# Router logits from the turned tokens and eight more columns of the second feed forward matrix, instead of turns of the normalised rows

## The chip, the cores and the metric

The kernel runs on one core of one Trainium2 chip. The core has a matrix engine (TensorE, PE in the profile; its weight loads are listed apart as PEld), a vector engine (VectorE, DVE), a scalar engine (ScalarE, ACT), GpSimd (POOL), and SyncE (SP), which here mostly issues transfers. On-chip data lies in SBUF, 128 partitions wide. Matmuls write to PSUM, which has eight banks of 512 float32 values for each partition. The metric is device time in microseconds, the median of several runs.

## The reference, cut to what matters

Two images of 256 channels and 56 by 56 pixels go through a convolutional neighbourhood attention (layer 0) and then, as 6272 tokens of 256 channels, through a linear attention with a feed forward part and through a mixture of eight experts (layer 1). The change lies in layer 1, between the feed forward part and the router:

```
# t: 6272 tokens of 256 channels; ln = (x - mean) / sqrt(var + 1e-5)
xn  = ln(t)                                     # input of the linear attention
msg = ln(attention(xn) @ Wm) * g1 + b1
h   = relu(concat([xn, msg]) @ W1)
t   = t + xn + ln(h @ W2) * g2 + b2             # token after the attention layer
x2  = ln(t)                                     # input of the experts
probs   = softmax(x2 @ Wr + br)                 # 8 experts
top_p, top_idx = top_k(probs, 2)
weights = top_p / sum(top_p)
xe  = ln(x2) * ln_g[e] + ln_b[e]
y   = gelu(xe @ W1[e] + b1[e]) @ W2[e] + b2[e]
out = t + sum of the two chosen y, weighted
```

The router needs `x2 @ Wr`. Since `x2` is `(t - mean) * r`, and a token `t` is the old token plus `xn` plus the feed forward result, the logits can also be summed from `xn @ Wr` and `h @ (W2 * g2) @ Wr`, if the columns of `Wr` are centred first.

## The kernel before, in words

**Stages.** The profile's span has three parts. Up to about 780 us the function `front` does the convolutions and the neighbourhood attention, and at its end `first_keys` starts the linear attention's keys for the first image. From about 780 to 1340 us `layer1` runs the linear attention, the feed forward part and the router over groups of tokens, and in its last quarter already the first expert tiles. From 1340 us on the remaining expert tiles run (`Experts.run`, lines 1388 to 1433).

**Tiles.** Tokens come in blocks of 128 rows. `order` (line 1452) has 14 groups: eleven of four blocks, two of two blocks, and one of a single block.

**The pipeline.** The loop at line 1830 takes steps s = 0 to 17. In step s, `queries` handles group s, `message` group s-1, `feed_forward` group s-2, `route` group s-3, and in steps 0 to 5 two `keys` generators handle blocks of the second image. Each of them is a generator that yields between parts. The strings `turns` and `last` (lines 1818 to 1823) are the order written out by hand in which the parts are taken: q, m, f, r, u and v (keys), p (what is left of the previous step's `route`), c (shared set-up of the experts) and e (a part of an expert tile). `manual_schedule` holds TensorE to this order. The orders of the other engines are set beforehand by a planner, which works with its own costs and takes first what is marked `high_priority`; every engine works its queue in order.

**What a group does.** `keys` (line 266) normalises two blocks (`stats`, `rstd`, `norm`), turns them (TensorE transposes into `pts`, copied by `evac` into `xT`) and forms the keys; on GpSimd it also replaces the stored token by token + normalised token + b2 (lines 286 to 289). `queries` multiplies `xT` by `w_q` and divides by a denominator. `message` forms `pm`, normalises it (`rms`, `rstd`, a ScalarE multiply) and turns it. `feed_forward` (line 1658) makes four tiles `p1` (16 matmuls of up to 512 columns, ScalarE Relu into `hT`), and then per two blocks eight matmuls into one bank `py` of 2 times 256 columns (line 1678), the sums of squares (`rms`, ScalarE), `rstd` (VectorE scale, then a power on GpSimd), `u` = py times its scale and g2 (VectorE, line 1687), the addition to the token (GpSimd, line 1691) and a write of the token to `y2` by SyncE. `route` (line 1732) takes statistics of the new token, normalises it twice in one go into `row`, turns `row` with eight transposes and two copies (lines 1755 to 1761), and in its second part multiplies the turned rows by `wr`, eight columns wide (line 1766); `top_two` picks the experts in some twenty small VectorE operations, the third part counts slots with two matmuls into `pp`, and the rest scatters the rows to their slots in device memory (`xs`) by GpSimd's indirect transfers.

**PSUM in this part.** `ps_h` has three banks for `pm`, `p1`, `py` and one of the expert accumulators (`py2`); `ps_q` two (queries, turned messages, expert `ph`); `ps_a` two (keys, `pts`, `pl`, `pp`); `ps_k` one. A tile waits until all readers of the bank's previous tile are done.

**Weights.** `layer1` loads its constants with GpSimd-issued transfers (`load`, line 1464). `prepare_feed_forward` centres the columns of W2 (`fw2`) after step 0. A matmul of float32 appears in the profile as two records, a transpose as one.

## Time and profile before

| what | value |
|---|---|
| median of 3 runs | 2046.03 us (2042.52 to 2046.82) |
| the profiled execution: its own time, its span | 2042.29 us, 2040.5 us |
| mean granted TensorE clock | 0.975 |
| busy in the span: PE, PEld, DVE, ACT, POOL | 92%, 66%, 50%, 31%, 33% |
| chain that ended last: PE, DVE, DMA, POOL | 66%, 14%, 6%, 5% |
| TensorE busy, 780 to 840 us | 54.82 of 60 us |
| TensorE busy, 1340 to 2040 us | 675.86 of 700 us |
| first and last `py` of the feed forward (L1678) | 845.3 and 1305.5 us |

A line of the timeline reads: start in us, duration in us, engine, line of the kernel, operation, output <- inputs with shapes, how many instructions were merged, and in brackets how long the engine had been idle before and what ended that. A line of the windows reads: stretch, its length, then busy time and number of instructions of each engine, the granted clock, the transfers' share and their rate. The durations of merged TensorE lines include the pipeline's depth; the time that a run of matmuls takes from the queue is the distance to the next line's start.

### The profile page before, as it was taken

What the parts mean: (1) busy time and instruction counts of PE and PEld (TensorE: products, weight loads), DVE (VectorE), ACT (ScalarE), POOL (GpSimd) and SP (SyncE); (2) the same over time, 40 slices, a digit from 0 to 9 for tenths busy, and PEclk for the clock granted to TensorE, in tenths of its full rate; (3) what the DMA queues carried; (4) which work ended last, traced back from release to release, by engine and by line L of the source; (5) the groups of instructions that cost most, each with busy time, mean ns of one, the idle gap of its engine ahead of it and who ended that gap; (6) DMA issues with size and microseconds to landing.
All of it is one profiled execution on the core that took longest, in us unless ns stands there. A gap on an engine that the chain in (4) does not pass through costs nothing.

```text
span 2040.5 us, 27636 instructions
## 1 busy us (share of the span) xinstructions
PE 1882.0 (92%) x10102; PEld 1342.9 (66%) x10102; DVE 1020.2 (50%) x2483; ACT 623.8 (31%) x1228; POOL 680.4 (33%) x772
## 2 busy tenths in 40 slices
PE   4999898999777888999999999999999999999995
PEld 2545454554445555666656667888888888888885
DVE  4987988877875566355555554342212221221121
ACT  1333334323232222333332323322222222222332
POOL 4532110121033235346344445533233332333221
PEclk9999899999889899999999999999999999999998
DMA  5542432344412224001011143577666767666995
GB/s 117 151 109 74 144 111 71 101 137 112 149 44 65 51 52 155 11 11 50 35 43 54 42 140 104 165 202 211 201 193 188 196 189 205 189 196 194 294 274 158
DMA packets 189911, 264.65 MB, mean 130 GB/s; under 512 B 26424, under 2 KB 149638, under 8 KB 189520
## 3 DMA queue, kind: packets, MB, share of 16 engines
q1 hardware_dynamic: 160912, 220.82, 35.5%
q0 software_dynamic: 20576, 29.75, 7.6%
q10 hardware_dynamic: 8272, 12.15, 1.7%
q8 instruction: 84, 1.38, 0.3%
q14 instruction: 67, 0.55, 0.1%
HBM read 196.38 MB, written 70.55 MB: 131 GB/s over the span
## 4 chain that ended last, share of the span: by engine, by line
PE 66%; DVE 14%; DMA 6%; POOL 5%; issue 3%; ACT 3%; SPq 1%; DVEq 0%; POOLq 0%; ACTq 0%
PE ph L1404 15%; PE py L1422 15%; PE pc L549 6%; PE py L528 5%; PE p L1666 5%; PE po L609 4%; PE s_ps L364 2%; DVE yc L567 2%; POOL rs L263 2%; PE s_ps L599 2%; DMA y<-yt,idi 2%; DVE p L604 2%; DMA xr<-xs 2%; PE kx L307 2%; PE kp L294 2%
## 5 line engine op out<-in xcount | busy, mean ns | idle before, releaser
L1404 PE MATMUL ph<-xe,w1e 128*128 128x256 f32 (+1 forms) x1696 | 362.6, 371 | 3.7 <-DVE xe L1380 2.5
L1422 PE MATMUL py<-w2e,hT 128*128 128x256 f32 x1616 | 359.0, 379 | 0.0
L1408 ACT ACTIVATE hT<-ph,sv 128x256 f32<-128x256 f32 (+1 forms) x424 | 196.5, 464 | 499.1 <-PE ph L1404 496.3
L1404 PEld LDWEIGHTS ph<-xe,w1e 128*128 128x128 f32 x1696 | 310.3, 191 | 46.1 <-DVE xe L1380 3.8
L1422 PEld LDWEIGHTS py<-w2e,hT 128*128 128x128 f32 x1616 | 302.5, 190 | 38.7
L567 DVE SCALAR_TENSOR_TENSOR yc<-ypad,w,yc 128x1120 f32<-128x1120 f32 x192 | 266.5, 1389 | 32.3 <-ACT yc L562 28.9
L161 POOL DMA_INDIRECT y<-yt,idi x101 | 160.8, 1592 | 230.2 <-DVE yt L1428 135.8
L549 PE MATMUL pc<-ypad,diag 128*128 128x448 f32 x432 | 176.8, 548 | 1.0 <-ACT ypad L534 1.0
L1360 DVE CAST idi<-xr 128x2 int32<-128x2 f32 (+1 forms) x53 | 10.5, 199 | 300.3 <-DMA xr<-xs 295.8
L528 PE MATMUL py<-t_a,wq 128*128 128x448 f32 (+1 forms) x384 | 150.1, 527 | 10.6 <-DVE t_a L503 10.3
L1428 DVE SCALAR_TENSOR_TENSOR yt<-py,eq,yt 128x256 f32<-128x256 f32 x101 | 48.6, 483 | 217.6 <-PE py L1422 217.4
L603 ACT ACTIVATE p<-s_ps 112x952 f32<-112x952 f32 (+5 forms) x88 | 102.1, 1160 | 148.2 <-PE po L609 81.2
L604 DVE TENSOR_TENSOR p<-p,tab 112x952 f32<-112x952 f32 (+5 forms) x88 | 125.1, 1425 | 30.6 <-ACT p L603 30.6
L263 POOL TENSOR_TENSOR rs<-rs,mhalf 128x2 f32<-128x2 f32 (+2 forms) x89 | 66.5, 753 | 217.5 <-DVE rs L262 155.2
L517 POOL TENSOR_SCALAR diag<-ident,w 128x128 f32<-128x128 f32 x108 | 89.1, 845 | 142.2 <-PE pc L549 125.4
L549 PEld LDWEIGHTS pc<-ypad,diag 128*128 128x128 f32 x432 | 79.8, 191 | 69.6 <-issue 64.4
L1386 POOL TENSOR_SCALAR yt<-b2e,eq 128x256 f32<-128x256 f32 x101 | 47.4, 478 | 218.8 <-DMA b2e<-in_L_ffn_b 212.6
L528 PEld LDWEIGHTS py<-t_a,wq 128*128 128x128 f32 x384 | 70.6, 194 | 75.0 <-issue 58.8
L161 POOL DMA_INDIRECT xs<-row,si x98 | 96.5, 985 | 58.3 <-DVE si L1790 26.4
L609 PE MATMUL po<-p,v 98*32 98x170 f32 (+5 forms) x960 | 77.0, 376 | 38.8 <-DVE p L604 17.1
L1666 PE MATMUL p<-m2T,fw 128*128 128x512 f32 (+2 forms) x224 | 93.9, 542 | 0.0
L1678 PE MATMUL py<-fw,hTl 128*128 128x256 f32 x392 | 88.5, 381 | 0.0
(364 smaller groups left out, 2550.0 us busy)
## 6 DMA issues: line engine op xcount, KB each, us to landing
w1e<-in_L_ffn_W SPq DMA_DIRECT2D x53, 1024.0 KB
w2e<-in_L_ffn_W SPq DMA_DIRECT2D x53, 1024.0 KB
yd<-yc SPq DMA_DIRECT2D x24, 784.0 KB
ld<-yd SPq DMA_DIRECT2D x28, 448.0 KB
xr<-xs SPq DMA_DIRECT2D x48, 260.0 KB
b2e<-in_L_ffn_b SPq DMA_DIRECT2D x53, 128.0 KB
yr<-y SPq DMA_DIRECT2D x11, 512.0 KB
td<-t_i SPq DMA_DIRECT2D x24, 224.0 KB
```

Source lines behind the costliest of these rows:

```text
L161: ins = nc.gpsimd.indirect_dma_start(out=dst[:, :], out_offset=bass.IndirectOffsetOnAxis(ap=index, axis=0), in_=src, in_offset=None, **kw,)
L263: newest[1] = nc.gpsimd.tensor_tensor(r[:, :n], r[:, :n], mhalf[:, :n], ALU.pow).ins
L528: nc.tensor.matmul(py[:, :n, :], wq1[:, ct, oc * P : (oc + 1) * P], x_sb[:, ct, (q0 + g0) * WW : (q0 + g0 + n) * WW], start=(ct == 0), sto ...
L549: nc.tensor.matmul(pc, diag[:, tap, :], ypad[:, dy : dy + 8, dx : dx + WW], start=(tap == 0), stop=(tap == 8),)
L567: nc.vector.scalar_tensor_tensor(yc[:, 8:, :], src, w, yc[:, 8:, :], ALU.mult, ALU.add)
L603: nc.scalar.activation(p[:nk, :, :n], s_ps[:nk, :, :n], AF.Exp)
L604: nc.vector.tensor_tensor(grid(p), grid(p), table[:nk], ALU.mult)
L609: nc.tensor.matmul(dst[hs] if w is None else den[hs], v[:nk, hs] if w is None else w[:nk, :], grid(p)[:, h, :, o : o + q.shape[2]], start= ...
L1404: nc.tensor.matmul(p1, x.w1[:, ct, j * P : (j + 1) * P], x.xe[:, ct, :], start=(ct == 0), stop=(ct == 1),)
L1408: nc.scalar.activation(hT[:, j, :], p1, AF.Gelu, bias=x.sv[:, 4 + j : 5 + j])
L1422: nc.tensor.matmul(py, hT[:, j, h * P : (h + 1) * P], x.w2[:, j, :], start=(j == 0), stop=(j == NJ - 1),)
L1666: nc.tensor.matmul(p1[:, :w], fw1[:, k, oc * P : (oc + 1) * P], rhs, start=(k == 0), stop=(k == 3))
```

## The change

The rows are no longer turned for the router. Part by part:

- `rstd` keeps variance + eps beside its result, and `keys` passes a place in a new tile `tk.up` (one value per token) into which GpSimd multiplies the two: the old token's standard deviation.
- W2 and g2 get eight more columns: `fw2` is 4 x 264, `g2` 264 wide with ones at its end. A new generator `prepare_router` runs in three parts (x) in step 1: it centres `wr`, scales it by g2 and by b2 (new tile `g2b2`, two small transfers), turns `fw2` with eight transposes and two copies, multiplies the turned matrix by the scaled `wr`, and copies the result into the eight columns.
- In `feed_forward` a block's `py` is 264 wide and has a bank of its own, so that two blocks take two banks; `u` carries the eight columns along, and a small addition makes `lb`.
- `wr` is padded to 32 columns. `route` multiplies it, as the stationary side, with the turned tokens `xT` that the keys made: block k writes partitions 32k to 32k+31 of one bank `pa`; one copy `la` and one transpose give the logits in `pl`.
- `top_two` has two more operations (times 1 + deviation, plus `lb`).
- Smaller: `xt` and `st` are smaller, `mn` has two buffers instead of three, and the order string of step 1 has three x.

```diff
-    def rstd(sm, var, scale):
+    def rstd(sm, var, scale, deviation=None):
         n = var.shape[1]
-        r = sm.tile([P, 4], F32, name="rs")
+        r = sm.tile([P, 2, 4], F32, name="rs")
...
+        if deviation is not None:
+            nc.gpsimd.tensor_tensor(deviation, r[:, 0, :n], r[:, 1, :n], ALU.mult)
+        return r[:, 0, :]
...
+            fw2 = wp.tile([P, 4, C + E], F32, name="fw2")
...
+            wr = wp.tile([P, 2, 32], F32, name="wr")
+            nc.gpsimd.memset(wr, 0.0)
...
+            def prepare_router():
+                ps = ps_a.tile([P, 512], F32, name="wrm", tag="a")
+                for ct in range(2):
+                    nc.tensor.matmul(ps[:, :E], ones, wr[:, ct, :E], start=(ct == 0), stop=(ct == 1))
...
+                yield
+                pt = [ps_a.tile([P, 512], F32, name="fwt", tag="a") for _ in range(2)]
+                f2T = wk.tile([P, 2, 512], F32, name="f2T", tag="qz")
+                for ct in range(2):
+                    for kk in range(4):
+                        nc.tensor.transpose(
+                            pt[ct][:, kk * P : (kk + 1) * P], fw2[:, kk, ct * P : (ct + 1) * P], ident
+                        )
+                    evac(f2T[:, ct, :], pt[ct])
+                yield
+                ps = ps_a.tile([P, 512], F32, name="fwr", tag="a")
+                for kk in range(4):
+                    for ct in range(2):
+                        nc.tensor.matmul(
+                            ps[:, kk * E : (kk + 1) * E], f2T[:, ct, kk * P : (kk + 1) * P], wg[:, ct, 0, :],
+                            start=(ct == 0), stop=(ct == 1),
+                        )
...
                 for k0 in range(0, n, 2):
                     kn = min(2, n - k0)
-                    py = ps_h.tile([P, 2, C], F32, name="py", tag="h")
+                    pys = []
                     for k in range(kn):
+                        py = ps_h.tile([P, 512], F32, name="py", tag="h")
+                        pys.append(py)
                         c0 = (k0 + k) * P
                         for kk in range(4):
                             nc.tensor.matmul(
-                                py[:, k, :], hT[:, kk, c0 : c0 + P], fw2[:, kk, :],
+                                py[:, : C + E], hT[:, kk, c0 : c0 + P], fw2[:, kk, :],
                                 start=(kk == 0), stop=(kk == 3),
                             )
...
+                    nc.vector.tensor_tensor(
+                        lb[:, k0 : k0 + kn, :], u[:, :kn, C:], b2r.unsqueeze(1).to_broadcast([P, kn, E]), ALU.add
+                    )
...
-                nc.vector.tensor_tensor(p, lg, bc(scale, E), ALU.mult)
+                nc.vector.tensor_tensor(p, lg, bc(up, E), ALU.mult)
+                nc.vector.tensor_tensor(p, p, lb[:, :n], ALU.add)
+                nc.vector.tensor_tensor(p, p, bc(scale, E), ALU.mult)
...
-            def route(n0, n):
+            def route(n0, n, lb):
+                xT = tk.turned(n0, n)
+                pa = ps_a.tile([P, 512], F32, name="pa", tag="a")
+                for ct in range(2):
+                    for k in range(n):
+                        nc.tensor.matmul(
+                            pa[32 * k : 32 * k + 32, :P], wr[:, ct, :], xT[:, ct, k * P : (k + 1) * P],
+                            start=(ct == 0), stop=(ct == 1), skip_group_check=True,
+                        )
+                la = wk.tile([P, P], F32, name="la", bufs=1)
+                evac(la[: 32 * n, :], pa[: 32 * n, :P])
...
-                pts = [ps_a.tile([P, 512], F32, name="pts", tag="a") for _ in range(2)]
                 for k in range(n):
                     last = norm(row[:, k, 0:C], t[:, k, :], mv, rs, k)
-                    turn(pts, k, row[:, k, 0:C])
...
-                x2T = tk.turned(n0, n)
-                for ct in range(2):
-                    evac(x2T[:, ct, :], pts[ct][:, : n * P])
                 yield
-                pl = ps_a.tile([P, 4, E], F32, name="pl", tag="a")
-                for k in range(n):
-                    for ct in range(2):
-                        nc.tensor.matmul(
-                            pl[:, k, :], x2T[:, ct, k * P : (k + 1) * P], wr[:, ct, :],
-                            start=(ct == 0), stop=(ct == 1),
-                        )
-                ohs = top_two(pl[:, :n], sd2, row, n)
+                pl = ps_a.tile([P, 4, 32], F32, name="pl", tag="a")
+                nc.tensor.transpose(
+                    pl.rearrange("p k e -> p (k e)")[:, : 32 * n], la[: 32 * n, :], ident[: 32 * n, : 32 * n]
+                )
+                ohs = top_two(pl[:, :n, :E], up, lb, r1, row, n)
...
-            turns = "quvuvuqv", "mquvmuvquv", "mqfpPPPPcufmuqfurfvrfvfv", "mwqfwpPPPPfwmqfrfrff"
+            turns = "quvuvuqv", "mxquvmxuvquxv", "mqfpPPPPcufmuqfurfvrfvfv", "mwqfwpPPPPfwmqfrfrff"
```

## The prediction

> **What bounds the kernel now.** First the page: which engine is busy, and where.

> ```profile
> PE 1882.0 (92%) x10102; PEld 1342.9 (66%) x10102; DVE 1020.2 (50%) x2483; ACT 623.8 (31%) x1228; POOL 680.4 (33%) x772
> ...
> PE   4999898999777888999999999999999999999995
> ```

> TensorE is busy almost throughout, but a mean says nothing of the stage that changes, so next the windows of that stage.

> ```profile
> 780.00:840.00 60.00, 54.82 (x212) 36.40 (x212) 34.88 (x83) 21.68 (x50) 29.39 (x33) 0.97 0.17 50
> 840.00:1000.00 160.00, 156.73 (x634) 106.58 (x633) 85.04 (x320) 55.74 (x139) 73.70 (x81) 1.00 0.08 27
> 1000.00:1160.00 160.00, 155.84 (x606) 100.21 (x605) 84.91 (x340) 52.31 (x139) 69.18 (x73) 1.00 0.14 48
> 1160.00:1240.00 80.00, 73.43 (x302) 50.84 (x300) 44.90 (x219) 23.72 (x72) 39.09 (x46) 0.96 0.34 115
> ```

> From 840 to 1160 us TensorE idles under 3%, at a granted clock of 1.00: work taken from it there is time, and so is every wait put into it. At 780 to 840 and 1160 to 1240 it waits for others about 8%. After 1340 it is busy 97% with expert tiles that do not change, so a shift arrives at the end. Third, the timeline of one plain step (step 9), which carries the sum.

> ```profile
> 1111.22 1.04 PE L1533 MATMUL pts<-ident,row 128*128 128x128 f32 x8
> ...
> 1112.10 1.88 PE L1666 MATMUL p<-xT_b,fw 128*128 128x512 f32 x4
> ...
> 1115.53 1.85 PE L1766 MATMUL pl<-wr,xT_b 128*128 128x8 f32 x16
> 1117.23 7.15 PE L1678 MATMUL py<-fw,hTl 128*128 128x256 f32 x32
> ...
> 1120.97 0.38 ACT L1528 ACTIVATE sq<-py 128x256 bf16<-128x256 f32 x1 [2.42 <-PE py L1678]
> ...
> 1122.18 0.16 DVE L262 TENSOR_SCALAR rs<-ssf 128x2 f32<-128x2 f32 x1
> 1122.49 0.72 POOL L263 TENSOR_TENSOR rs<-rs,mhalf 128x2 f32<-128x2 f32 x1 [7.30 <-DVE rs L262]
> 1123.25 0.87 DVE L1687 SCALAR_TENSOR_TENSOR u<-py,rs,g 128x256 f32<-128x256 f32 x2 [0.91 <-POOL rs L263]
> ...
> 1124.22 3.62 PE L1636 MATMUL pm<-mw,qz 128*128 128x256 f32 x16
> ```

> The distances of starts give the prices: turns 0.88, logits 1.70, `py` 6.99, `pm` 3.46 (to the next line, 1127.68). Watch the bank: `py` began at T = 1117.23, its second block's sums end at 1121.95, and `u` starts 1.30 later. A bank is held until `u`. Nobody waits for it now, since three banks serve two `py` tiles.

> **The change part by part** (differences, against the profiled execution's 2042.29: span 2040.5 and 1.8 around it; this is 3.7 below the median of the runs, 2046.03, onto which the sum is set).

> *Less matmul work in a group of four.* Out: 0.88 + 1.70 = 2.58. In: eight `pa` matmuls, 16 records of 128 columns. Without overlap each lasts like a turn, 0.109 (0.88 / 8): 1.75. The nearest row with 32-column weights in four column places is the attention of layer 0:

> ```profile
> 595.13 0.99 PE L609 MATMUL po<-p,v 98*32 98x221 f32 x16 [1.65 <-issue]
> ...
> 595.91 0.40 PE L609 MATMUL po<-p,ones 98*32 98x221 f32 x4
> ```

> Sixteen records of 221 columns take 0.78 to the next start; scaled to 128 columns 0.45, unscaled 0.78. I take 0.55, ends 0.45 and 1.75. One transpose, 0.11. `py` wider by 8/256 of 6.99: 0.22. Net 2.58 - 0.55 - 0.11 - 0.22 = 1.70 less. Groups of two: 1.25 out, 0.65 in; of one: 0.2 less.

> [...]

> *The banks, steps 6 to 10.* A block's `py` now has a bank of its own: two blocks hold two of the three, and the fourth block must wait until the first's `u` is through. First block done at T+1.8; the second's sums end at T+4.33 (3.61 + 0.24 latency + 0.48); `u` starts 1.30 later, ends at T+6.1. TensorE wants the bank at 3 x 1.805 = T+5.41: wait 0.8 with a semaphore. The fourth block then ends at T+8.0; its `u` pair starts at T+10.0 and frees the third bank at T+10.5; the second `pm` wants it at T+9.7: another 0.8. Together 1.6. VectorE's top-two operations run in the same stretch (T+0.2 to T+4.84) and get 0.45 longer (two at 0.225); if the scale before the power is queued behind them, the first wait is 1.65 and both are 2.5. Both orders occur in the trace (behind at 1122.18, in their middle at 1220.73): I take 2.0. Five steps at 2.0 - 1.7 = +0.3: **+1.5** (ends -0.5 and +4.0).

> *Steps 2 to 5.* Here 1.73 of `kp` matmuls lie between the two `py` pairs (890.94 to 892.66), so the fourth block comes at T+7.1, after T+6.1: no wait. If that cover went, 0.8 a step. Three steps at -1.7 and one with only the wider `py`: **-4.9**.

> *Step 11.* VectorE's queue stands behind the first expert tile's rows:

> ```profile
> 1188.76 0.23 DVE L1358 TENSOR_SCALAR eq<-xr,etmA 128x2 f32<-128x2 f32 x1 [3.25 <-DMA xr<-xs]
> ...
> 1194.12 0.16 DVE L262 TENSOR_SCALAR rs<-ssf 128x2 f32<-128x2 f32 x1
> 1194.36 0.72 POOL L263 TENSOR_TENSOR rs<-rs,mhalf 128x2 f32<-128x2 f32 x1 [8.52 <-DVE rs L262]
> 1195.11 0.88 DVE L1687 SCALAR_TENSOR_TENSOR u<-py,rs,g 128x256 f32<-128x256 f32 x2 [0.84 <-POOL rs L263]
> ```

> Behind it wait the top-two, `rs` and `u`. In this step `py` ran from 1186.85 to 1193.84; shortened it starts at 1184.95, and the fourth block waits from 1190.4 to 1196.0, ending at 1197.9: +4.1. With `rs` ahead of the top-two, -1.1. The row is nearer to the first: **+2.5**.

> *Steps 12 to 16.* Step 12: 1.7 less, but `u` ended at T+7.6 and the fourth block wants T+5.5, 2.1 more; then TensorE stood 4.5 for `chosen` and `before`, and takes up the difference: 0 (ends -1.5, +1.5). Step 13: 1.8 less, but the first `p1` (T+4.6) needs a bank of `py`, free at T+6.2: -0.2 (-1.8, +0.5). Steps 14 to 16: 1.4 less, of which the longer top-two takes part, since TensorE waited for `chosen` there (1.66 and 1.96): -0.6 (-1.4, +0.9). **-0.8**.

> *The preparation, step 1.* Third part 20 records at 0.109 = 2.18, of which 0.65 lies in the wait before `pm` at 818.04; eight transposes 0.87, then 0.6 until a copy frees a bank for `kp`; the first part, 0.44, hides in the 0.88 wait for `xt`. 3.0, and 0.8 for VectorE, on which TensorE waits five times in this step, with eight small operations and one copy (0.69): **+3.8** (2.0, 6.5).

> *What I cost at nothing.* GpSimd: 25 small multiplications, between the 0.11 of a small memset and the 0.72 of a power; before the next work in `first_keys` it idles mostly 3 to 7 us. Without that cover up to 0.7 a call. Two more transfers and two memsets, 1.4 (0.71 each) + 0.3 on GpSimd ahead of the token updates at 781.98; its next urgent power, at 797.39, came after 6.6 idle; uncovered 1.7. VectorE a step: `sd`, half of two copies (0.85) out; `r1`, `up`, two small operations, two `lb`, half of `la`, wider `u` in, together 1.2; it is 53% busy, and the slots were ready 13 us before `pp` (1121.9 to 1134.55). `mn` with two buffers: its last reader is 25 us ahead. `f2T` takes a `qz` buffer already read by the step's first part. SyncE's writes of tokens follow the addition, up to 2 us later, and nothing reads them soon.

> **Sum**: 3.8 - 4.9 + 1.5 + 2.5 - 0.8 = **+2.1**: 2044.4 for the profiled execution, 2048 on the median. All low ends give -9, all high ends +13.

> **The rivals.**
> *Slower by queues.* `rs` stays behind the top-two in every step. The two waits then exceed 1.7, the point that decides: 4.0 in steps 6 to 10, 4.1 in step 11, 1.5 in step 12, 5 for the preparation, -4.9, -0.8: +9, 2055. For it: the order at 1122.18; against: 1220.73.
> *Faster.* The planner lets `rs` through at once, the preparation hides: -0.5 - 1.1 - 1.5 + 2.0 - 4.9 - 1.5 = -7.5, 2038.5. For it: TensorE idles 8% around both ends of the stage; against: even then a step's banks cost 1.6.
> *The overlap fails.* `pa` costs 1.75: 1.2 in nine groups, +11, 2059. Against it the `po` row.

> **How the numbers follow.** A difference under 0.2%, 4.1 us, can't be told from none here. Forecast 0.42 (0.02 faster, 0.30 same, 0.10 slower), slower by queues 0.31 (0.04 same, 0.27 slower), faster 0.21 (0.18 faster, 0.03 same), overlap failing 0.06 (slower): faster 0.20, same 0.37, slower 0.43. The range goes from the faster rival's 2038 to the overlap's 2059; the forecast's own is 2043 to 2053.

> **What would show it.** `pa`: 16 records to the next start in 0.45 to 0.8. A plain step, 34.58 long before, is 34.5 to 35.4. TensorE waits for `u` (line of `py`) before the fourth block and before the second `pm`, 0.7 to 1.7 each, in steps 6 to 10 and not in 3 to 5, which shorten by 1.7 from 42.2. In step 1 the queue is 2 to 6.5 longer. Wrong would be: no wait for `u`, a step under 33.5, or new waits of TensorE for VectorE elsewhere.

## The result and the profile after

The changed kernel takes 2056.85 us (median of 5 runs, 2053.42 to 2058.95) against 2046.03 (2041.24 to 2049.60) beside it: a ratio of 1.0056, 95% interval 1.0036 to 1.0076, about 11 us slower. The forecast of 2048 was too low. Its own range of 2043 to 2053 did not hold the time; the wide range of 2038 to 2059, whose ends are those of two rivals, did, near its upper end. The profiled execution took 2056.2 us, its span is 2054.3.

The page of the changed kernel, busy time by engine and TensorE in 40 slices:

```profile
PE 1877.4 (91%) x10050; PEld 1325.1 (65%) x10050; DVE 1024.5 (50%) x2552; ACT 617.4 (30%) x1222; POOL 688.8 (34%) x801
...
PE   4999898999778888999999988999999999999996
```

TensorE is busy 4.6 us less than before (1882.0), and the kernel is longer. The windows of the stage (stretch, length, busy time and count of TensorE, weight loads, VectorE, ScalarE, GpSimd; granted clock, transfers):

```profile
780.00:840.00 60.00, 54.54 (x241) 38.74 (x240) 35.91 (x92) 20.83 (x48) 30.83 (x41) 0.97 0.20 67
840.00:1000.00 160.00, 152.37 (x601) 99.79 (x600) 86.30 (x324) 52.68 (x135) 75.06 (x85) 0.99 0.08 27
1000.00:1160.00 160.00, 150.58 (x570) 87.43 (x569) 85.57 (x359) 50.45 (x134) 71.11 (x73) 1.00 0.15 48
1160.00:1240.00 80.00, 68.88 (x276) 45.15 (x274) 41.44 (x209) 21.73 (x70) 34.45 (x40) 0.96 0.33 108
```

From 840 to 1160 TensorE idles 17.0 us where it idled 7.4. The same work, from the first `py` of step 2 to that of step 14, before and after:

```profile
845.25:1303.99 458.74, 442.85 (x1850) 308.59 (x1849) 238.12 (x1005) 156.12 (x400) 214.84 (x234) 0.99 0.20 64
851.38:1318.01 466.63, 431.85 (x1774) 286.19 (x1773) 239.76 (x1058) 149.69 (x393) 218.99 (x240) 0.98 0.20 63
```

TensorE is busy 11.0 us less and idle 18.9 us more (34.8 against 15.9): the matmul work went, as forecast, and waits put back more than it was worth. Where the time stayed is read from the first `pm` of each step, with which a step begins, in both timelines (us):

| stretch | before | after | difference | forecast |
|---|---|---|---|---|
| start to the turned keys `kxt` (the front) | 762.50 | 765.12 | +2.6 | 0 |
| `kxt` to step 2 (the preparation) | 54.19 | 58.72 | +4.5 | +3.8 |
| steps 2 to 5 | 167.33 | 167.97 | +0.6 | -4.9 |
| steps 6 to 10 | 174.79 | 174.49 | -0.3 | +1.5 |
| step 11 | 35.03 | 40.04 | +5.0 | +2.5 |
| step 12 to the end | 846.66 | 847.96 | +1.3 | -0.8 |
| span | 2040.5 | 2054.3 | +13.8 | +2.1 |

In the experiments a step goes from its first `py` to the next one's, so that other orders of the parts can be compared; "step 11 to 14" is then 117.14 before and 127.27 after, "step 2 to 6" 168.23 and 168.08, "step 6 to 11" 173.37 and 171.28.

Step 9 of the changed kernel in the timeline answers to the lines of step 9 shown before:

```profile
1119.15 0.65 PE L1807 MATMUL pa<-xT_b,wr 128*32 128x128 f32 x16
...
1123.26 0.27 PE L1839 MATMUL pl<-ident,la 128*128 128x128 f32 x1
...
1123.37 5.51 PE L1742 MATMUL py<-fw,hTl 128*128 128x264 f32 x24
...
1128.19 0.16 DVE L263 TENSOR_SCALAR rs<-ssf 128x2 f32<-128x2 f32 x1
...
1129.26 0.49 DVE L1751 SCALAR_TENSOR_TENSOR u<-py,rs,g 128x264 f32<-128x264 f32 x1 [0.78 <-POOL rs L264]
...
1129.90 2.02 PE L1742 MATMUL py<-fw,hTl 128*128 128x264 f32 x8 [1.02 <-DVE cnt L1850]
...
1131.75 1.89 PE L1696 MATMUL pm<-mw,qz 128*128 128x256 f32 x8
...
1134.21 1.97 PE L1696 MATMUL pm<-mw,qz 128*128 128x256 f32 x8 [0.57 <-ACT sq L1588]
```

`pa` takes 0.57 to the next line, `pl` 0.11, the fourth block of `py` waits 1.02 and the second `pm` 0.57. The name behind the first wait is `cnt`, VectorE's neighbour in the queue; the bank is free when the first `u` is through, at 1129.75. `rs` stands in VectorE's queue ahead of the last two top-two operations, and comes 0.5 after the squares that it needs (ready at 1127.66). From step 6 to 10 a step lasts 34.56 to 34.68, before 34.58 to 34.59: what the smaller work saves, 1.6 of new waits takes back.

Step 11:

```profile
1190.74 5.51 PE L1742 MATMUL py<-fw,hTl 128*128 128x264 f32 x24
...
1196.09 0.23 DVE L1361 TENSOR_SCALAR eq<-xr,etmA 128x2 f32<-128x2 f32 x1 [3.19 <-DMA xr<-xs]
...
1201.05 0.16 DVE L263 TENSOR_SCALAR rs<-ssf 128x2 f32<-128x2 f32 x1
...
1202.04 0.49 DVE L1751 SCALAR_TENSOR_TENSOR u<-py,rs,g 128x264 f32<-128x264 f32 x1 [0.71 <-POOL rs L264]
...
1202.68 3.86 PE L1742 MATMUL py<-fw,hTl 128*128 128x264 f32 x8 [6.44 <-DVE cnt L1850]
...
1206.34 2.95 PE L1696 MATMUL pm<-mw,qz 128*128 128x256 f32 x8
```

VectorE stands at 1196.09 for the rows `xr`; the top-two, `rs` and `u` queue behind it, and TensorE waits 6.44 for the bank. Then the eight records of the fourth block need 3.86 instead of 2.02. The next view says why: windows as long as the first half-rate stretch in it, 3.41 us, laid around the start of that spell and of another.

```profile
914.91:918.33 3.42, 3.42 (x10) 1.47 (x9) 2.15 (x7) 0.05 (x1) 3.34 (x5) 1.00 0.00 0
918.33:921.74 3.41, 1.27 (x9) 0.75 (x7) 3.38 (x12) 1.27 (x2) 2.35 (x3) 1.00 0.00 0
921.74:925.15 3.41, 2.83 (x7) 2.30 (x8) 1.45 (x5) 0.00 (x0) 2.13 (x2) 0.50 0.11 39
925.15:928.57 3.42, 3.42 (x11) 1.69 (x10) 1.98 (x5) 1.23 (x2) 2.59 (x3) 1.00 0.32 117
...
1198.22:1201.64 3.42, 0.00 (x0) 0.00 (x0) 2.77 (x21) 1.10 (x6) 0.35 (x1) 1.00 1.05 379
1201.64:1205.05 3.41, 2.37 (x6) 1.88 (x7) 1.85 (x8) 0.00 (x0) 1.64 (x2) 0.50 0.49 162
1205.05:1208.46 3.41, 3.41 (x9) 2.66 (x8) 1.01 (x7) 0.47 (x2) 0.71 (x1) 0.50 0.84 215
```

In the second line TensorE is busy 1.27 of 3.41 us, through two waits, 1.03 and 1.69 long. In the third the granted clock is 0.50, and in the fourth 1.00 again. The same after the wait of step 11, there for two windows, 6.83 us together. (A spell is a stretch at a clock of 0.50 without a break; one of 6.83 us counts as two windows.) By an estimate from this length and this clock, a window at half rate loses up to 1.71 us, half of 3.41, and less where TensorE waits in it. From 840 to 1345 us the changed kernel loses up to 10.2 us in this way, the kernel before 5.1 (the shortfall of the granted clock, summed over windows of 0.5 us).

### The profile page after: what moved, and what is told of

It is laid out like the page before. It is cut to its first block, busy times and chain, and to the rows that moved or that the text cites. A ratio compares the mean times of both kernels' runs of the same rounds, so it can differ in the third digit from the quotient of the medians.

```text
span 2054.3 us, 27710 instructions
## 1 busy us (share of the span) xinstructions
PE 1877.4 (91%) x10050; PEld 1325.1 (65%) x10050; DVE 1024.5 (50%) x2552; ACT 617.4 (30%) x1222; POOL 688.8 (34%) x801
## 3 DMA queue, kind: packets, MB, share of 16 engines
q1 hardware_dynamic: 160912, 220.82, 35.1%
## 4 chain that ended last, share of the span: by engine, by line
PE 69%; DVE 13%; DMA 6%; POOL 3%; ACT 3%; issue 3%; SPq 0%; ACTq 0%; DVEq 0%; POOLq 0%
PE ph L1407 16%; PE py L1425 15%; PE p L1726 7%; PE pc L552 6%; PE py L531 5%; PE po L612 4%; PE s_ps L367 2%; DVE yc L570 2%; DVE p L607 2%; DMA y<-yt,idi 2%; PE kx L310 2%; PE s_ps L602 2%; PE kp L297 2%; POOL rs L264 2%; PE pm L1696 2%
## 5 line engine op out<-in xcount | busy, mean ns | idle before, releaser
L531 PE MATMUL py<-t_a,wq 128*128 128x448 f32 (+1 forms) x384 | 148.8, 523 | 12.2 <-DVE t_a L506 10.2
L1742 PE MATMUL py<-fw,hTl 128*128 128x264 f32 x392 | 93.8, 393 | 12.0 <-DVE cnt L1850 11.5
```

What stands on the lines that cost most here:

```text
L531: nc.tensor.matmul(py[:, :n, :], wq1[:, ct, oc * P : (oc + 1) * P], x_sb[:, ct, (q0 + g0) * WW : (q0 + g0 + n) * WW], start=(ct == 0), sto ...
```

## The experiments

All times are beside the kernel before on the same chip, in five rounds; stretches are from the profiled execution. "Changed" is the kernel after.

**E1, banks alone** (on the kernel before).

```diff
-                    py = ps_h.tile([P, 2, C], F32, name="py", tag="h")
+                    pys = [ps_h.tile([P, 512], F32, name="py", tag="h") for k in range(kn)]
...
-                                py[:, k, :], hT[:, kk, c0 : c0 + P], fw2[:, kk, :],
+                                pys[k][:, :C], hT[:, kk, c0 : c0 + P], fw2[:, kk, :],
```

> The kernel before with one part of the change alone: each block's py has a PSUM bank of its own (still 256 columns, no eight columns; logits still from the turned rows). Theory (the banks are the dearest part): TensorE waits for VectorE's u before the fourth block, 1.0 to 1.3 us, and before the second pm, 0.5 to 0.8 us, in each of steps 6 to 10, so these steps are 36.2 to 36.6 us instead of 34.58; step 11 has a wait of 5 to 7 us before its fourth block, step 13 one of 1 to 2 us before p1. Together 8 + 6 + 1.5 = about 15 us more than before (ratio 1.006 to 1.009). Rival (the waits come from VectorE's longer queue, two more top-two operations and the wider u, and not from the banks): under 0.5 us a step, steps 6 to 10 at 34.6 to 35.1 us, at most 4 us in all (ratio under 1.002).

2052.81 against 2044.45, ratio 1.0038 (1.0025 to 1.0051): 8.4 us, where the theory asked for about 15 and the rival for at most 4. Timeline of TensorE, step 9 and step 11:

```profile
1127.91 1.99 PE L1678 MATMUL py<-fw,hTl 128*128 128x256 f32 x8 [0.73 <-DVE u L1687]
...
1132.11 1.99 PE L1636 MATMUL pm<-mw,qz 128*128 128x256 f32 x8 [0.47 <-DVE u L1687]
...
1201.60 3.78 PE L1678 MATMUL py<-fw,hTl 128*128 128x256 f32 x8 [4.53 <-DVE u L1687]
```

Steps 7 to 10 are 35.91 each, 1.33 longer. From step 11 to 14 it takes 123.70, 6.6 more than before, with the wait of 4.53 and two windows at half rate around its end. So the banks alone make most of the waits, 1.20 of 1.59. The rest is the rival's: with two top-two operations fewer, VectorE comes to `rs` 4.56 us after the step's first `py` (1126.31), in the changed kernel 4.82 (1128.19).

**E2, preparation alone** (on the kernel before; its results go to tiles of their own).

```diff
...
-            turns = "quvuvuqv", "mquvmuvquv", "mqfpPPPPcufmuqfurfvrfvfv", "mwqfwpPPPPfwmqfrfrff"
+            turns = "quvuvuqv", "mxquvmxuvquxv", "mqfpPPPPcufmuqfurfvrfvfv", "mwqfwpPPPPfwmqfrfrff"
...
-                    mn = wk.tile([P, 2, C], F32, name="mn", bufs=3)
+                    mn = wk.tile([P, 2, C], F32, name="mn")
```

> The kernel before with the preparation alone: the three parts in step 1, the two small transfers and mn with two buffers; its results go to tiles that nobody reads. Theory: TensorE's extra 3.3 us of matmul work and a few waits lengthen steps 0 and 1 by 3 to 4.5 us, nothing else moves: ratio 1.0015 to 1.0025, steps 2 to 5 at 42.2 us as before. Rival (the 3.4 us seen there in the changed kernel are a lower granted clock and chance): under 1.5 us, ratio under 1.001.

2049.68 against 2044.45, ratio 1.0030 (1.0018 to 1.0042). From `kxt` to the first `py` of step 2 it takes 85.47, 2.7 more; steps 2 to 6 take 168.24, as before (168.23). But 1.2 of the 2.7 is there already at 776.55, ahead of the preparation, where this execution has two windows at half rate (from 769.48) and the kernel before one. So the preparation itself takes about 1.5 here, half of the theory's 3 to 4.5 and at the rival's bound of 1.5; nothing moves in steps 2 to 5, as the theory says. The whole is more than its stretch: the profiled execution has 3.1 more between steps 11 and 14 and 2.4 more after that, which no part of the edit explains; how much of it is chance was not settled.

**E3, copies dealt out as before** (on the changed kernel).

```diff
-                evac(la[: 32 * n, :], pa[: 32 * n, :P])
+                evac(la[: 32 * n, :], pa[: 32 * n, :P]); evac_n[0] += 1
```

> The changed kernel, but the counter that deals the copies out between ScalarE and VectorE is advanced twice for the one copy la, so that every step deals them out alike, as in the kernel before. Theory (one copy fewer per group moves the keys' copy xT_b to VectorE in every second step, behind the row's operations, and so eats what steps 3 to 5 should have gained): the waits for xT_b, slot and qz in steps 3 to 5 go, these steps are 40.3 to 41 us instead of 42.2 on average, 4 to 5 us less in all than the changed kernel, ratio to the kernel before about 1.003. Rival (GpSimd's order, with the new small multiplications and a token update ahead of the router's power, holds VectorE up): the waits for qz stay near 1 us a step, within 1.5 us of the changed kernel, ratio 1.005 to 1.006.

2056.55 against 2044.45, ratio 1.0066 (1.0053 to 1.0079): no gain. The wait for `xT_b` went from 1.69 to 0.75, and step 3 to 4 from 44.86 to 42.71, with the half-rate spell that no longer follows it. The waits for `qz` stayed (1.43, 1.06, 0.93). So the copies were not the cause of most of what TensorE's timeline of the changed kernel shows in steps 3 to 5:

```profile
878.13 0.98 PE L1593 MATMUL mts<-ident,mn 128*128 128x128 f32 x7 [1.40 <-DVE qz L247]
...
922.32 3.38 PE L297 MATMUL kp<-w_k,xT_b 128*128 128x256 f32 x8 [1.69 <-DVE xT_b L177]
...
964.53 0.98 PE L1593 MATMUL mts<-ident,mn 128*128 128x128 f32 x7 [0.90 <-DVE qz L247]
```

**E4, another order in steps 6 to 10** (on the changed kernel: `pd` between the `py` pairs, `pq` between `py` and `pm`).

```diff
-            turns = "quvuvuqv", "mxquvmxuvquxv", "mqfpPPPPcufmuqfurfvrfvfv", "mwqfwpPPPPfwmqfrfrff"
+            turns = "quvuvuqv", "mxquvmxuvquxv", "mqfpPPPPcufmuqfurfvrfvfv", "qmwfwpPPPPfwmfrfrfqf", "qmfpPPPPcfmfrfrfqf"
...
```

> The changed kernel with another order of TensorE's parts in steps 6 to 10: the denominator's two matmuls (pd) lie between the two py pairs, and the next step's queries (pq) between py and pm. Theory (the waits in these steps are for banks held until u, and anything put in between covers them): no wait before the fourth block and the second pm, steps 7 to 10 at 32.9 to 33.3 us, 8 us less in all than the changed kernel, ratio to the kernel before about 1.0015. Rival (VectorE is the limit of a step, its queue late by its own work): the waits move to qz before pm or to pp, the steps stay at 34 to 34.7 us, 0 to 3 us gained.

2050.48 against 2044.45, ratio 1.0036 (1.0023 to 1.0050): about 4 us gained, half of what the theory asked. From step 6 to 8 the steps are 32.00 and 32.47, shorter than the 32.9 to 33.3 that it names; then waits come back, and step 11 still has one of 4.43 before its fourth block. Two lines of TensorE, steps 8 and 10 to 11:

```profile
1085.40 2.02 PE L1742 MATMUL py<-fw,hTl 128*128 128x264 f32 x8 [1.30 <-DVE cnt L1850]
...
1158.29 0.67 PE L1696 MATMUL pm<-mw,qz 128*128 128x256 f32 x2 [3.13 <-DVE qz L1670]
```

In step 11 the new order ends with `pm` straight behind `py`, while `pd` had just been moved ahead of it: `qz` is late by 3.13 and 0.59, and a spell at half rate follows (1160 to 1163.5). In step 8 ScalarE's first square of `py` came at 3.33 us after the start of `py` instead of 1.98 in step 7, which makes `u` late; what delayed it stays open.

**E5, the router's power earlier** (on the changed kernel).

```diff
-                    nc.vector.tensor_copy(r1, rs)
...
-                nc.vector.tensor_tensor(rs, rs, rs2, ALU.mult)
+                rs = rr; nc.vector.tensor_tensor(rr, r1, rs2, ALU.mult)
...
         nc.gpsimd.tensor_tensor(t, t, tk.b2.unsqueeze(1).to_broadcast([P, n, C]), ALU.add)
+        nc.gpsimd.tensor_tensor(tk.up[:, n0 : n0 + n], rk[:, 0, :n], rk[:, 1, :n], ALU.mult)
```

In the changed kernel GpSimd does a deviation (0.20) and a token update (0.78) ahead of the router's power at 873.70. Before, that power came straight behind a power of the keys, at 866.92. The step's other lines lie 5.81 later in the changed kernel, so its power is 0.97 late.

> The changed kernel with two small edits that bring the router's power on GpSimd forward: the copy of rs ahead of it on VectorE is gone (the product goes to a tile of its own instead), and the multiplication that keeps the old deviation stands behind the update of the stored tokens. Theory (in steps 3 to 5 the router's power is issued about 1 us later than before, behind the deviation and one token update, so VectorE's rows and qz are late and TensorE waits for qz): the waits for qz before the turned messages fall from 1.40, 1.03 and 0.90 us to under 0.6, the one for xT_b (1.69) goes too, steps 2 to 5 are 163 to 166 us together (to the py of step 6) instead of 168.1, 2 to 5 us less than the changed kernel; ratio to the kernel before 1.003 to 1.005. Rival (it is the length of VectorE's queue, not the moment of the power): waits and steps as in the changed kernel, 1.0055 to 1.0065.

2060.57 against 2045.42, ratio 1.0075 (1.0062 to 1.0089). The profiled execution is by far the fastest of the six (2051.91; the others 2057.94 to 2062.70), so it doesn't show where the median's loss lies. In it the waits for `qz` are gone, as the theory says, and three others stand in their place:

```profile
868.60 0.67 PE L278 MATMUL pts<-ident,xt 128*128 128x128 f32 x4 [2.03 <-DVE xt L148]
...
910.74 0.67 PE L278 MATMUL pts<-ident,xt 128*128 128x128 f32 x4 [1.67 <-DVE xt L148]
...
953.12 0.83 PE L278 MATMUL pts<-ident,xt 128*128 128x128 f32 x4 [1.74 <-DVE xt L148]
```

From step 2 to 6 it takes 167.69, 0.4 less than the changed kernel. The power's moment makes the waits for `qz`, but with it moved TensorE waits for VectorE's `xt` instead: the time is not got back, so the theory of this one cause falls, and with it half of the rival, since the waits did move.

**E6, the first expert tile's rows later** (on the changed kernel).

```diff
+            x.rest = lambda: self.rest(x, tab, k)
+            if not later:
+                x.rest()
+            return x
...
-            nxt = self.fetch(*ts[0], pools)
+            nxt = self.fetch(*ts[0], pools, getattr(pools, "later", 0) > 0)
             yield
+            for _ in range(getattr(pools, "later", 0)):
+                yield
+            if hasattr(pools, "later"):
+                nxt.rest()
+                yield
...
```

> The changed kernel with one thing moved: VectorE's and GpSimd's few operations on the first expert tile's rows are put into the queues after step 11's u, the transfer itself stays. Theory (step 11's wait is made by VectorE standing for xr, behind which top-two, rs and u queue): the wait before the fourth block falls from 6.44 to 1.0 to 1.7 us, step 11 to 12 is 31 to 32 us instead of 36.36, 4 to 5.5 us less than the changed kernel, ratio to the kernel before 1.0025 to 1.004. Rival (the lost time comes back, since step 12 has waits for the slots and for the same transfer that are now met earlier): step 12 grows by what step 11 gains, total within 1.5 us of the changed kernel.

2052.43 against 2045.42, ratio 1.0033 (1.0017 to 1.0049). Step 11 in TensorE's timeline, the second line the wait before its fourth block:

```profile
1197.58 4.27 PE L1754 MATMUL py<-fw,hTl 128*128 128x264 f32 x18 [1.60 <-ACT hTl L1741]
...
1203.20 2.02 PE L1754 MATMUL py<-fw,hTl 128*128 128x264 f32 x8 [1.35 <-DVE cnt L1862]
```

It fell from 6.44 to 1.35, with no spell behind it; a wait of 1.60 for `hTl` stands new ahead of it. Step 11 to 12 is 30.28 instead of 36.36. A part comes back, step 12 to 13 is 38.31 instead of 35.91; from step 11 to 14 it takes 123.63, 3.6 less than the changed kernel. The cause of the long wait is shown; the rival is right on some 2.4 us of it. (This profiled execution, 2057.37, is the slowest of nine.)

**E7, a second order** (on the changed kernel: `pq` between the `py` pairs, `pd` in the next step, `pm` after the second `p1`).

```diff
-                out.append(qz)
...
-            turns = "quvuvuqv", "mxquvmxuvquxv", "mqfpPPPPcufmuqfurfvrfvfv", "mwqfwpPPPPfwmqfrfrff"
+            turns = "quvuvuqv", "mxquvmxuvquxv", "mqfpPPPPcufmuqfurfvrfvfv", "mwfwpPPPPfwmfrfrfqf", "dfpPPPPcfmfrfmrfqf", "dfpPPPPcqfmfrfrfmqf"
...
```

> The changed kernel with another order of TensorE's parts in steps 6 to 11: the next queries (pq, 3.4 us) lie between the two py pairs, the denominator's matmuls (pd) open the next step, and pm comes after the second p1. Theory (the bank waits of steps 6 to 10 are covered by 3.4 us of other matmuls, more than the 1.0 needed, and qz is no longer wanted at once as it was with pd in between): no wait over 0.3 us for u, cnt or qz in steps 7 to 10, these steps at 32.3 to 33 us instead of 34.6, 8 to 11 us less in steps 6 to 10; step 11 as before or up to 4 us better or worse; ratio to the kernel before 0.9995 to 1.002. Rival (VectorE's queue is the limit of the step): new waits for qz, mn or m2T, steps at 33.5 us and more, ratio 1.003 to 1.006.

2074.61 against 2045.42, ratio 1.0141 (1.0125 to 1.0157). Neither theory nor rival had this wait, in step 6 to 7 of TensorE's timeline:

```profile
1047.21 3.01 PE L1726 MATMUL p<-xT_a,fw 128*128 128x512 f32 x4 [4.48 <-ACT mn L1706]
```

A `pm` bank is held until `mn`, behind a square, a scale, a power and a multiply. In the old order `pq` (3.43) lies behind `pm`; here two `p1` do, and they need these banks. Behind each such wait came a spell at half rate (from 1048.03, 1085.57, 1123.12 and 1160.66; the clock is 0.50 in the 3.41 us from 1048.03), and a step is 37.8 to 38.9.

**E8, three edits together**: E5, E6 and E7.

> The changed kernel with the three edits together: the prompt power in steps 2 to 5, pq between the py pairs in steps 6 to 10, the first expert tile's rows after step 11's u. Theory (three separate causes, so the gains add): 14 to 20 us less than the changed kernel, ratio to the kernel before 0.995 to 0.999, faster than the kernel before. Rival (VectorE's queue is the common cause and a gain at one place is lost at the next): 0 to 8 us less, ratio 1.001 to 1.005.

2076.83 against 2045.42, ratio 1.0154 (1.0136 to 1.0172). E7's wait is 5.66 here. The run says that E7's order outweighs the two edits that it is joined to, and no more.

**E9, the bank freed early** (on the changed kernel).

```diff
                     for k in range(kn):
-                        rms(pys[k][:, :C], ss[:, k0 + k : k0 + k + 1])
+                        nc.scalar.copy(u[:, k, :], pys[k][:, : C + E])
+                        rms(u[:, k, :C], ss[:, k0 + k : k0 + k + 1])
...
-                            u[:, k, :], pys[k][:, : C + E], rs[:, k : k + 1], g2, ALU.mult, ALU.mult
+                            u[:, k, :], u[:, k, :], rs[:, k : k + 1], g2, ALU.mult, ALU.mult
...
```

> The changed kernel, but ScalarE first copies each block's py, all 264 columns, into u, and the squares and VectorE's scaling work on the copy, in place: the bank is free as soon as it is copied, and no longer held until u. Theory (the waits of steps 6 to 13 are the time that a bank is held): ScalarE frees a bank some 0.7 us after its sums end, so the waits before the fourth block (1.02) and the second pm (0.57) go in steps 6 to 10, which become 32.9 to 33.3 us; in step 11 the copies still stand behind the router's Exp on ScalarE and through it behind xr, so 3 to 5 of 6.4 us stay; step 13's 1.3 goes. Together 9 to 13 us less than the changed kernel, ratio to the kernel before 0.9995 to 1.001. Rival (VectorE's queue is the limit of a step, a freed bank only shows the next wait): steps 34 us and more, 0 to 4 us gained.

2053.21 against 2044.28, ratio 1.0044 (1.0029 to 1.0060). The profiled execution is the fastest of nine (2045.46, up to 2059.07). No wait for `u` is left in its steps 6 to 10, and yet the steps from 7 to 10 are 36.44, 34.01 and 34.80. Step 8 in TensorE's timeline:

```profile
1068.63 0.33 PE L1593 MATMUL mts<-ident,mn 128*128 128x128 f32 x1 [0.95 <-DVE qz L247]
...
1069.30 0.98 PE L1593 MATMUL mts<-ident,mn 128*128 128x128 f32 x7 [0.34 <-DVE qz L247]
...
1070.85 3.59 PE L1665 MATMUL pd<-qz,ksm 128*128 128x512 f32 x4 [0.57 <-ACT m2T L175]
```

TensorE now arrives earlier at the turned messages and waits 0.95 and 0.34 for `qz`, then 0.57 for `m2T`, and at 1071.08 half rate begins. The rival is right: a freed bank shows the next wait. In step 11, 1.70 of the 6.44 is left.

**E10, copies on ScalarE** (E9, and the keys' `xT` and `la` copied by ScalarE alone).

```diff
-        evac(xT, pts[:, :, : n * P])
+        nc.scalar.copy(xT, pts[:, :, : n * P])
...
```

> The same, and in addition the copies xT of the keys and la are all made by ScalarE, none by VectorE. Theory (VectorE's order of work, one instruction late behind another, keeps steps 3 to 5 near 42 us): with about 1.4 us of copies a step off it, the waits for qz (1.40, 1.03, 0.90) and for xT_b (1.69) get shorter by half or more, and the way from the first py of step 2 to that of step 6 is 164 to 166.5 us instead of 168.1. Rival (these steps follow GpSimd's powers, on which VectorE itself waits): the way stays at 167 to 169 us, or gets longer where ScalarE is late.

2056.89 against 2044.28, ratio 1.0051 (1.0034 to 1.0069). From step 2 to 6 it takes 168.77; the waits for `qz` are 1.43, 1.06 and 0.93, in E9 1.43, 1.07 and 0.93. These copies on VectorE are not what holds steps 3 to 5. The rival's 167 to 169 us is met; that the cause is GpSimd's powers, as it says, is not shown.

**E11, E9 and E6 together.**

> The bank freed early by ScalarE's copy, and the first expert tile's few operations on VectorE and GpSimd put behind step 11's u. Theory (two separate causes, both needed in step 11): no wait over 1 us in step 11, whose way to step 12's py is 28 to 30.5 us instead of 36.4, steps 6 to 10 at 32.9 to 33.3 us, 13 to 18 us less than the changed kernel, ratio to the kernel before 0.997 to 0.999. Rival (what step 11 gains comes back in steps 12 and 13): within 2 us of the kernel with the early bank alone.

2053.32 against 2044.28, ratio 1.0043 (1.0027 to 1.0060). Step 11 to 12 is 26.98, with no wait over 1 us, better than the theory asked. But step 6 to 11 takes 174.85, 3.6 more than in the changed kernel, with two spells at half rate. On the whole nothing is gained over E9.

**E12, other work in the gaps** (on the changed kernel: E6; E4's order in steps 6 to 9, with step 10 leading back to the old one; in step 1 the transposes of `fw2` ahead of the turned messages).

```diff
-            turns = "quvuvuqv", "mxquvmxuvquxv", "mqfpPPPPcufmuqfurfvrfvfv", "mwqfwpPPPPfwmqfrfrff"
+            turns = "quvuvuqv", "mxquvxmuvquxv", "mqfpPPPPcufmuqfurfvrfvfv", "qmwfwpPPPPfwmfrfrfqf", "qmfpPPPPcfmfrfrfqf", "qmfpPPPPcfmqfrfrff"
...
-                    for part in turns[3 if s == 6 else min(s, 2)] if s < ng - 2 else last[s - ng + 2]:
+                    for part in turns[5 if s == 10 else 4 if 7 <= s <= 9 else 3 if s == 6 else min(s, 2)] if s < ng - 2 else last[s - ng + 2]:
```

> The changed kernel with three things moved: in steps 6 to 9 pd lies between the py pairs and pq between py and pm (in step 10 pq stays ahead of pm and pd goes back to its place); the first expert tile's few operations on VectorE and GpSimd stand behind step 11's u; in step 1 the eight transposes of fw2 stand ahead of the turned messages. Theory (the lost time is waits that cluster, and a half-rate spell of the granted clock of 3.4 us, 1.7 lost, behind each stretch of some 3.4 us in which TensorE was busy about half): steps 7 to 10 at 32 to 34 us, no wait of 3 us for qz, step 11 without the wait of 6.44 and without its two half-rate spells, 8 to 13 us less than the changed kernel, ratio to the kernel before 0.999 to 1.002: as fast as the kernel before, and not faster, since the preparation's 3 us and steps 3 to 5 stay. Rival (each gain is given back by the next wait, as with the two edits of the order tried so far): 0 to 5 us less, ratio 1.003 to 1.0055.

2036.79 (2033.36 to 2039.81) against 2045.50, ratio 0.9963 (0.9949 to 0.9977): faster than both kernels. TensorE in step 8, and the fourth block of step 11:

```profile
1077.55 3.73 PE L1754 MATMUL py<-fw,hTl 128*128 128x264 f32 x16
...
1081.11 1.88 PE L1677 MATMUL pd<-qz,ksm 128*128 128x512 f32 x4
...
1082.83 3.72 PE L1754 MATMUL py<-fw,hTl 128*128 128x264 f32 x16
...
1086.39 3.60 PE L1668 MATMUL pq<-xT_b,w_q 128*128 128x512 f32 x8
...
1089.82 3.99 PE L1708 MATMUL pm<-mw,qz 128*128 128x256 f32 x16
...
1093.65 1.88 PE L1738 MATMUL p<-xT_b,fw 128*128 128x512 f32 x4
...
1187.21 2.02 PE L1754 MATMUL py<-fw,hTl 128*128 128x264 f32 x8 [1.72 <-DVE cnt L1862]
```

Step 8 has no bracket of a wait: `pd` lies in front of the second pair, `pq` in front of `pm`. From step 6 to 9 the steps are 32.00, 32.02 and 32.03 long, 2.6 less than before. Step 9 to 10, the way back to the old order, is 37.58: it holds two `pd`, a wait of 1.03 for `m2T` and a window at half rate. Step 11 waits 1.72, and no spell follows (the granted clock stays 1.00). Against the changed kernel, step 2 to 11 is 7.0 shorter (332.39 against 339.36), step 11 to 14 9.2 shorter (118.10), `kxt` to step 2 0.5. From step 2 to 14 TensorE is idle 21.8 us, in the changed kernel 34.8, and the shortfall of the granted clock is 6.8 against 10.2: of the 16.1 gained there, 13.0 are waits and some 3 the clock. Another 3.3 of the 20.2 between the two spans lie in the front, whose matmuls are the same. It beat its own expectation of "as fast as before". The three moves were not run apart in this form. E4 and E6 gave about 4 us each; E4 left the wait of step 11 and made one of 3.13, and E6 left those of steps 6 to 10. Whether the kernel before would gain from such moves too was not tried.

## Why the prediction was right or wrong

**The matmul terms: right.** `pa` was taken at 0.55 and measures 0.57; the transpose 0.11 and 0.11; the 16 records in four column places overlap (0.57, where 1.75 was worked out for one after the other), so the rival "the overlap fails" is out. The lines ahead of and behind `pa` are 0.1 longer to the next start than their like: 1.81 and 1.82, in step 9 of the kernel before 1.71 and 1.72. That is 0.2 a group that the sum did not have.

**The banks, steps 6 to 10: right in place, too dear by 0.4 a step.** Two waits, before the fourth block and the second `pm`, were forecast at 0.7 to 1.7 each; they are 1.02 and 0.57. The sum of 1.6 is the low end: most of the top-two lies ahead of `rs`, but holds it up by only 0.5. E1 gets waits of this kind from the banks alone. The step is 34.6, as forecast (34.5 to 35.4).

**The preparation: right in its sum.** +3.8 forecast, with 2.0 and 6.5 as the ends; measured +4.5 to step 2's first `pm` and +3.5 to its first `py`. E2, with about 1.5 to the same `py`, gives the preparation alone less than half of that; what makes the rest in the changed kernel is not shown.

**Steps 2 to 5, -4.9: wrong, and the largest miss.** The step that failed is "Three steps at -1.7": it looked for waits for `u` alone, and there are none. But TensorE, arriving earlier, met VectorE: its waits in these steps add up to 7.59 us, before to 3.84, among them 1.40, 1.03 and 0.90 for `qz` and 1.69 for `xT_b` (the lines are at E3). Before, the waits for `qz` were 0.60, 0.24 and under 0.15:

```profile
871.52 0.98 PE L1533 MATMUL mts<-ident,mn 128*128 128x128 f32 x7 [0.60 <-DVE qz L246]
...
913.79 0.98 PE L1533 MATMUL mts<-ident,mn 128*128 128x128 f32 x7 [0.24 <-DVE qz L246]
```

A half-rate spell of up to 1.71 came on top. That is up to 5.5 back for the 4.9 of work taken out. The prediction had named "new waits of TensorE for VectorE elsewhere" as a sign of being wrong, and here they are. "What I cost at nothing" has a share in it: GpSimd's small multiplications and the copy of `rs` did push the router's power back by 1 us, and E5 removed the waits for `qz` by undoing it. But E5, E3 and E10 did not get the time back; each moved the wait to `xt`, took away the spell alone, or left it. What chain holds these steps at 42 us is open: neither the dealing of the copies nor their share of VectorE's work settles it.

**Step 11, +2.5, and steps 12 to 16, -0.8: mechanism right, sizes wrong.** The cause was named with its row: VectorE at the rows of the first expert tile, with top-two, `rs` and `u` behind it. The high end had a wait of 5.6 for the fourth block; it is 6.44, and E6 shows that it is this queue. The step that failed is the choice of the value: the row spoke for the high end of +4.1, and the forecast took something in between; measured are +5.0. And no term of the sum, high ends included, had the clock. Between step 11 and step 14 the changed kernel has five half-rate windows (up to 8.5 us lost), the kernel before one (1.7), and some of that lies in step 12 and after.

**The front, +2.6: within chance.** The changed kernel and E4 have the same instructions in the same order there; the keys start at 765.12 in one and at 761.09 in the other, and these 4.0 us are there by 550 us. The granted clock adds a spread of its own: its shortfall from 640 to 780 us is 10.2 in the kernel before, 15.4 in the changed kernel, and 8.5 to 17.1 over the fourteen profiled executions.

**The rivals.** "Slower by queues" has the sum (2055), but by another way. `rs` has the same place in steps 6 to 11, behind all but two of the top-two operations. In steps 6 to 10 these are nearly through when the squares are ready (`rs` at 1128.19, squares at 1127.66), so the two waits stay under 1.7; in step 11 they are not (1201.05 and 1198.87). "Faster" had the low end of the banks, and fell with the gain in steps 2 to 5 and with step 11. What decided is the 18.9 us of new waits from step 2 to 14, of which no rival had those of steps 2 to 5, and with them the clock, which was in none: its shortfall there is 10.2 where it was 3.4. The runs agree: in 57 of the kernel before beside the experiments the mean granted clock is 0.969 to 0.977, and a straight line through them gives 1.25 us for each 0.001. The changed kernel's five runs have 0.968 or 0.969, 0.004 below the mean of the 57, so by this estimate some 5 of its 11 us go with the lower clock.

## What to carry to other kernels

A wait had two prices here, its length and the half-rate window (3.41 us at a clock of 0.50) that came behind some clusters of waits, so look at the granted clock behind each cluster before a sum is made. Matmul work taken from an engine that was 97% busy was worth here only what the next queue let through (11.0 us less busy, 18.9 more idle); after each removal ask what TensorE will now arrive too early for. Where a tile needs a bank for longer, put other work of the same engine into the gap, as in E12; freeing the bank, as in E9, brought up the next wait.

## What the runs showed of the hardware

Waits alike were followed by a spell or by none. In the changed kernel a wait of 1.76 for `chosen`, up to 1306.37, has the spell from 1307.45 behind it; in the kernel before one of 1.66 for the same tile, up to 1294.34, has none, though TensorE was busy 1.75 of 3.41 us from 1291.22 on (the clock is 1.00 there and from 1294.63 to 1298.04). In E7 TensorE was busy 1.53 of 3.41 us from 1041.20 on, and the clock stayed 1.00; in the next 3.41 us it was busy 0.82, and then the clock was 0.50. In E11 a spell begins at 796.75, behind 3.41 us in which TensorE was busy about 3.06. So E12's theory, a spell behind each stretch of some 3.4 us in which TensorE was busy about half, is wider than what the runs show; what decides is open.
